# Order and number of loads, held gather numbers and deeper buffers in a two-layer transformer with mixtures of experts

## The chip, the cores and the metric

The kernel runs on one core of a Trainium2 chip, as one launch. The metric is device time in microseconds (us) of that core, as the median of several runs. A core has five engines that work side by side, each on its own queue of instructions: TensorE (PE in the profile; its weight loads are listed as PEld), VectorE (DVE), ScalarE (ACT), GpSimd (POOL) and SyncE (SP). SP only issues transfers (DMAs); ACT and POOL can issue some too. An engine takes its instructions strictly in order, so an instruction that waits for a semaphore holds everything behind it on that engine.

## The reference, cut to what matters

Eight sequences of 512 tokens with 256 numbers each pass through two pre-norm blocks, each an attention and a mixture of experts:

```python
x = x + _L0_attn_ref(_layernorm(x), Wq, Wk, Wv, Wo)          # 16 heads of 16, 4 key heads, rotary, causal
x = x + _L0_ffn_ref(_layernorm(x), router_w, w_gate, w_up, w_down)
x = x + _L1_attn_ref(_layernorm(x), w_qkv, b_qkv, w_out, b_out)
x = x + _L1_ffn_ref(_layernorm(x), gate_w, w1, w2, w3, sw1, sw2, sw3)
```

The first mixture has 32 experts with 96 inner numbers, of which each token takes the 8 likeliest, with their weights normed to one. The second has 16 experts with 176 inner numbers, of which each token takes 2, and a shared expert with 352 inner numbers that every token passes through. An expert is the same in both:

```python
h = jax.nn.silu(x @ wg) * (x @ wu)
acc = acc + h @ wd * w_e[:, None]
```

All numbers are float32.

## The kernel before, in words

**Stages.** The program runs through four stages: attention 0 (to about 417 us), mixture 0, or MoE 0 (to about 871), attention 1 with the shared expert (to about 1427) and MoE 1 (to the end). In an attention stage a pipeline works on sequence after sequence. At the end of a sequence `route` chooses the experts and POOL scatters the normed rows of its tokens, each chosen token once for each of its experts, into a table `xg` in DRAM that is ordered by expert (L401). A row carries the numbers, the expert weights and the row number to which its result goes.

**Experts.** A MoE stage is run by `all_experts` (L1352) and `experts` (L1078). The sequences are split into two parts with tables of their own (`SPLIT`: four and four in MoE 0, six and two in MoE 1), so that the first part can start while the last sequences are still routed. A job is two tiles of 128 rows. There are 75 jobs a part in MoE 0, and 30 and 14 in MoE 1. Each job passes through five stages at fixed lags of whole steps: `load` (SP fetches the rows into `xg_m`, L1113, 7 buffers, lag 0), `turn_x` (TensorE transposes them into `xgT`, VectorE copies them to `xgTs`, L1122 and L1124, lag 4), `gate_up` (matmuls `gu`, L1155, ACT's SiLU, VectorE's product `h`, L1147, lag 5), `turn_h` (transposes `hT`, copy `hTs`, L1175 and L1176, lag 6) and `down` (matmuls `y`, L1186, lag 7). TensorE's order in it is the written order; the other engines' instructions are placed by a scheduler, which works with priorities and modelled times while the program is built.

**Results of a job.** ACT copies `y` to `ys` (L1191, 4 buffers). In MoE 0 SP stores `ys` in the table's own order (L1193). In MoE 1 POOL scatters it to the rows of its tokens (L1197), two scatters a job, for which VectorE takes the row numbers out of the loaded rows into a small tile `to` (L1132 to L1135, 5 buffers) at the start of `gate_up`.

**Weights.** The gate and up weights are loaded during the attention before. The down weights `dw` are loaded by `load_down` (L1255 to L1264), which `all_experts` calls ahead of `experts`: one transfer for each expert or piece of one that lies in one block of 128 rows, 48 in MoE 0 and 52 in MoE 1. They all stand on SP's queue.

**Work beside the jobs.** `Beside` runs other work a few steps at a time between the jobs. In MoE 0 that is the table of part 1, the weights of the next attention and, once part 0 is done, `gathers` (L1214) for sequences 0 to 3. `gathers` computes on VectorE the rows in which a token's eight results lie (`ykey` L1220 and L1221, `ykeys` L1224, `yrows` L1226), then POOL fetches them and adds them to `x_a` (L1229, 32 transfers a sequence). Sequences 4 to 7 are gathered during attention 1. In MoE 1 it is `results` (L1286): x comes back from DRAM as `x_c` (L163), two gathered tiles `g` (L1294) are added to it (L1305), TensorE transposes it (`xout`, L1315), ACT copies it to `xo` (L1316, one buffer) and SP stores it (L1317).

**x between stages.** A ring of five x tiles holds sequences in work (`new_x`). `keep_x` (L160) stores a sequence to DRAM, `fetch_x` (L163) brings it back. After attention 1 all eight are stored, the last by `x_kept` (L1388).

**The start.** `fast0` (L805) begins attention 0. On ACT's queue stand the loads of the q weights (L810), then the k weights (L819), cos and, behind the copy of the k weights, the v weights and sin (L830). SP has the identity, the router's weights `rw` and the biases (L201 to L204), and then x of sequence 0 (L1269). `issue_after(a)` lets the scheduler place an instruction only behind `a`.

Of the kernel before, what the change touches and what calls it, by code (L numbers as in the profile page):

```python
# [1 line left out]

# [5 lines left out]
F32 = mybir.dt.float32  # L8
# [82 lines left out]
def two_blocks_kernel(  # L91
# [106 lines left out]
        yield  # L198

    rw = cpool.tile([P, ND * (E0 + E1)], F32, tag="rw", name="rw")  # L200
    nc.sync.dma_start(out=rw[:, : ND * E0], in_=r0)  # L201
    nc.sync.dma_start(out=rw[:, ND * E0 :], in_=r1)
    bias1 = cpool.tile([P, BBW], F32, tag="bias1", name="bias1")
    nc.sync.dma_start(out=bias1, in_=b1)  # L204


    tpool = ctx.enter_context(tc.tile_pool(name="tiles", bufs=1, reuse_waits="tile"))
# [595 lines left out]
        return v1[:, t, : heads * (DH + 1)].rearrange("p (h d) -> p h d", d=DH + 1)[:, :, :DH]  # L803

    def fast0(awp, lnp, atp, late, ptp, ps, bank):  # L805
        ahead = {0: read_x(0, lnp)}
        wq = awp.tile([P, ND, D + 2 * HKV * DH], F32, tag="wqkv", name="wqkv0")
        lo, hi = A0["q"]
        q_in = lnp.tile([P, hi - lo], F32, tag="xT", name="q_in")
        nc.scalar.dma_start(out=q_in, in_=a0[:, lo:hi])  # L810
        q_in = q_in.rearrange("p (k m s g r) -> p k m s g r", k=ND, m=2, s=2, g=NG)
        for k in range(ND):
            q_out = wq[:, k, :D].rearrange("p (m g s d) -> p m g s d", m=2, g=NG, s=2)
# [261 lines left out]
            for item in self.items:  # L1075
                drain(item[3])

    def experts(n, gu, dn, mp, ps, again, beside):  # L1078

        name = f"m{n}{'g' * again}"  # L1080
        jobs = [(lay, i) for lay in lays[n] for i in range(0, lay.tiles(again), 2)]
# [45 lines left out]
        def gate_up(lay, i):  # L1127
            part = lay.part
            xT, xg = made.pop(("xT", part, i)), made.pop(("xg", part, i))
            h = mp.tile([P, 2, inner], F32, tag="h", name=f"h_{name}_{part}_{i}")  # L1130
            if n:
                to = made["to", part, i] = mp.tile([P, 2], I32, tag="to", name=f"to_{name}_{part}_{i}", bufs=5)  # L1132
                for j in range(2):

                    nc.vector.tensor_scalar(  # L1135
                        to[:, j : j + 1], xg.bitcast(I32)[:, j, D + lay.n_e :][:, bass.ds(offs[part, i + j][2], 1)],
                        -1.0, None, ALU.add,
                    )
            if n == 0:
                whole = ps.tile([P, 2, 2 * inner], F32, tag="gu", name=f"gu_{name}_{part}_{i}")  # L1140
                gus = [whole[:, 0, :], whole[:, 1, :]]
            else:
                gus = [ps.tile([P, 2 * inner], F32, tag="gu", name=f"gu_{name}_{part}_{i + j}") for j in range(2)]

            def scaled(j):

                nc.vector.scalar_tensor_tensor(  # L1147
                    h[:, j, :], h[:, j, :], xg[:, j, D:][:, bass.ds(offs[part, i + j][2], 1)], gus[j][:, inner:],
                    ALU.mult, ALU.mult,
                )  # L1150

            for j in range(2):
                at = offs[part, i + j][0]
                for c in range(ND):
                    nc.tensor.matmul(  # L1155
                        gus[j], xT[:, j, c, :], gu[:, bass.ds(at + c * 2 * inner, 2 * inner)],
                        start=(c == 0), stop=(c == ND - 1),
                    )
# [20 lines left out]
        def down(lay, i):  # L1179
            part = lay.part  # L1180
            hT = made.pop(("hT", part, i))
            y = ps.tile([P, 2, D], F32, tag="y", name=f"y_{name}_{part}_{i}")
            for j in range(2):
                at = offs[part, i + j][1]
                for q, (lo, n_in) in enumerate(chunks):
                    nc.tensor.matmul(  # L1186
                        y[:, j, :], hT[:n_in, q, j, :], dn[:n_in, bass.ds(at + q * D, D)],
                        start=(q == 0), stop=(q == n_ch - 1),
                    )
            ys = mp.tile([P, 2, D], F32, tag="ys", name=f"ys_{name}_{part}_{i}", bufs=4)  # L1190
# [16 lines left out]
        with tc.manual_schedule(engines={ENG.PE}):  # L1207
            for s in range(len(jobs) + stages[-1][1]):
                for stage, lag in stages:
                    if 0 <= s - lag < len(jobs):  # L1210
                        stage(*jobs[s - lag])
                beside.step(s)
            beside.finish()

    def gathers(b, gat, again=""):

        lay = lay_of(0, b)
        n_e, k, name = lay.n_e, lay.k, f"{again}_{b}"
        key = gat.tile([P, NT, n_e], F32, tag="ykey", name=f"ykey{name}", bufs=1)
        nc.vector.tensor_tensor(key, lay.keys[b], lay.shift.unsqueeze(1).to_broadcast([P, NT, n_e]), ALU.add)  # L1220
# [34 lines left out]
    def load_down(w, src, inner, routed):  # L1255

        chunks = -(-inner // P)
        width = inner // chunks
        for n, lo, hi, e, at in pieces(inner, routed):
            while lo < hi:  # L1260
                q, r = at // width, at % width
                rows = min(hi - lo, width - r)
                to = (e * chunks + q) * D
                nc.sync.dma_start(out=w[r : r + rows, to : to + D], in_=src[n][lo : lo + rows, 2 * ND * P :])  # L1264
                lo, at = lo + rows, at + rows

    def read_x(b, tmp, bufs=1):
        xf = tmp.tile([P, ND, T], F32, tag="xf", name=f"xf{b}", bufs=bufs)
        nc.sync.dma_start(out=xf, in_=x_in[b])  # L1269
        return xf  # L1270

    def load_x(b, tmp, bank, xf=None):
# [12 lines left out]
    def results(seqs, gat, op, ps, again="", behind=lambda: None):  # L1285


        def begin(b):
            fetch_x(b, x_after[1], f"c1{again}")
            lay = lay_of(1, b)  # L1290
            made[b] = [gat.tile([P, NT, D], F32, tag="gath", name=f"g1{again}_{b}_{i}", bufs=2 * K1) for i in range(K1)]
            for i in range(K1):
                lo = (i * len(lay.seqs) + b - lay.seqs[0]) * T
                nc.sync.dma_start(out=made[b][i], in_=lay.yg[lo : lo + T, :].rearrange("(p t) d -> p t d", t=NT))  # L1294
                yield
# [3 lines left out]
        for b, after in zip(seqs, [*seqs[1:], None]):  # L1299
# [11 lines left out]
            for c in range(ND):  # L1311
# [2 lines left out]
                for t in range(NT):  # L1314
                    nc.tensor.transpose(tr[:, t * P : (t + 1) * P], xs[b][:, t, c * P : (c + 1) * P], ident)  # L1315
                nc.scalar.copy(xf[:, c, :], tr)  # L1316
            nc.sync.dma_start(out=out[b], in_=xf)  # L1317

    def drain(part):
        for _ in part:  # L1320
# [32 lines left out]
    def all_experts(n, gw, gat, again=False, weights=()):  # L1353
# [6 lines left out]
        with ExitStack() as s:  # L1360
# [3 lines left out]
            ps = s.enter_context(tc.tile_pool(name=f"ps_m{n}{g}", bufs=2, space=PSUM, reuse_waits="tile"))  # L1364
            inner, chunks, src, routed = (I0, 1, f0, N0) if n == 0 else (I1, ND1, f1, N1R)
            dw = dwp.tile([P, lays[n][0].n_e * chunks * D], F32, tag="dw", name=f"dw{n}{g}")
            load_down(dw, src, inner, routed)

            def bank(name):
                return ps.tile([P, T], F32, tag="y", name=name)  # L1370
# [1 line left out]
            def x_in_ring():  # L1372
                for b in range(SPLIT[0]):
                    fetch_x(b, x_after[0], f"a1{g}")
                yield
                for b in range(SPLIT[0]):
                    yield from gathers(b, gat, g)

            def x_kept():
                with tc.issue_after(beside.load):  # L1380
                    keep_x(NB - 1, x_after[n])
                yield

            def weights_loaded():
# [7 lines left out]
            end = first + second + 6  # L1392
            beside = Beside()
            beside.add(2, min(34, first - 4), 6 + lays[n][1].n_e // 8, tables(lays[n][1], small, bank, again, beside))
            if not again:
                beside.add(8, 9, 1, x_kept())
            beside.add(
                first // 2, end, len(weights), weights_loaded(),
# [1 line left out]
            if n == 0:  # L1400
                beside.add(done, end, SPLIT[0] * 16 + 1, x_in_ring())
            else:
                beside.add(
                    done + 2, end, SPLIT[1] * 6, results(range(SPLIT[1]), gat, gat, ps, g, lambda: beside.last)
                )
            experts(n, gw, dw, mp, ps, again, beside)
            return beside.last


# [26 lines left out]
    with ExitStack() as s1:  # L1436
# [4 lines left out]
        with ExitStack() as s:  # L1441
# [15 lines left out]
            def after1(b):  # L1457
# [3 lines left out]
                xT = yield from turned(xn, lnp, bank, name)  # L1461
                yield from route(1, b, xn, xT, name, False)
                yield from shared(w1["s"], xT, xs[b], name)
                if b < NB - 1:
                    keep_x(b, x_after[1])
                if b == SPLIT[1] - 1:
                    yield from tables(lays[1][0], smp, bank, False)
# [38 lines left out]
    def general1(gat):  # L1506
        with ExitStack() as s:
# [20 lines left out]
            def all_of(b, name):  # L1528
# [8 lines left out]
                keep_x(b, x_after[1])  # L1537

            for b in range(NB):
                drain(all_of(b, f"f1g_{b}"))  # L1540
# [175 lines left out]
```

## Time and profile before

| What | Value |
|---|---|
| Median of 3 runs | 1705.02 us (1702.58 to 1710.43) |
| The profiled execution | 1707.52 us |
| Its span | 1705.8 us |
| Mean granted clock of TensorE | 0.962 |
| Scatters of rows to the experts (POOL, L401) | 320, 321.5 us busy |
| Gathers of MoE 0's results (POOL, L1229) | 256, 403.8 us busy |
| Gate and up matmuls (PE, L1155) | 1552, 339.1 us busy |
| Down matmuls (PE, L1186) | 952, 238.4 us busy |
| Loads of job rows (SP, L1113) | 388 of 144 KB |
| Bytes read and written in DRAM | 133.42 and 125.37 MB |

Times of the profile are counted from the start of the span. A row such as `start, length, engine, line, operation, out<-in xN` stands for N instructions of one kind that follow each other on their engine. What stands in brackets behind it is how long the engine had been idle before the first, and what ended that. A profile is of one execution, and its own time stands beside its span.

### The profile page before, as it was taken

The numbers are of one execution on the slowest core, as the hardware profiler recorded it, in microseconds if no ns is written. First come the engines' busy times: TensorE is split into PE (matmuls) and PEld (weight loads), VectorE is DVE, ScalarE is ACT, GpSimd is POOL, SyncE is SP. The second block draws the span as 40 slices with busy tenths as digits, with TensorE's granted clock in tenths as the row PEclk, the third lists the DMA queues.
The fourth block names the chain that finished last, engine by engine and source line by source line (L and its number), as shares of the span: only waits on it lengthen the run. The fifth ranks groups of instructions, "written<-read, shape, count | busy, mean of one in ns | idle before, by whom it ended". The sixth has DMA issues, their size and how long they took to land.

```text
span 1705.8 us, 31140 instructions
## 1 busy us (share of the span) xinstructions
PE 1551.6 (91%) x10180; PEld 1034.3 (61%) x10180; DVE 995.5 (58%) x3179; ACT 650.1 (38%) x865; POOL 822.4 (48%) x686
## 2 busy tenths in 40 slices
PE   5899999994999999999989999999899989999884
PEld 2355544543898999899863454544444445777663
DVE  5687887875555555555555765754656544444353
ACT  2555554552232333333334454454455331222222
POOL 0026777477710003888888548888511012333333
PEclk9999999997899999999999999999999999999997
DMA  2035557236988768999985345665312025353353
GB/s 73 13 87 155 163 166 269 97 138 197 303 255 259 212 200 216 265 274 274 275 188 71 44 109 80 128 139 72 84 53 84 25 92 168 99 160 106 120 186 143
DMA packets 246618, 257.84 MB, mean 151 GB/s; under 512 B 80907, under 2 KB 225425, under 8 KB 246452
## 3 DMA queue, kind: packets, MB, share of 16 engines
q1 hardware_dynamic: 189508, 165.73, 32.1%
q0 software_dynamic: 56448, 89.18, 22.6%
q8 instruction: 87, 1.43, 0.4%
q10 hardware_dynamic: 496, 0.85, 0.2%
q14 instruction: 79, 0.65, 0.1%
HBM read 133.42 MB, written 125.37 MB: 152 GB/s over the span
## 4 chain that ended last, share of the span: by engine, by line
PE 47%; POOL 19%; issue 14%; DVE 10%; DMA 5%; ACT 2%; SPq 2%; POOLq 0%; DVEq 0%; ACTq 0%
POOL x_a L1229 15%; PE gu_m L1155 7%; PE st_a L654 7%; PE o_a L677 6%; PE y_m L1186 4%; PE qkv_a L859 3%; PE xgT_m L1122 2%; POOL yg L1197 2%; PE sg_f L418 2%; POOL xg L401 2%; ACT p_a L659 2%; DVE p_a L665 2%; PE y_a L743 2%; PE su_f L418 2%; PE sy_f L431 2%
## 5 line engine op out<-in xcount | busy, mean ns | idle before, releaser
L1229 POOL DMA_INDIRECT x_a<-yg,yrows x256 | 403.8, 1577 | 279.9 <-DMA xg_m<-xg 184.5
L401 POOL DMA_INDIRECT xg<-xn_f,rows_f x320 | 321.5, 1005 | 413.7 <-DVE xn_f L396 177.6
L659 ACT ACTIVATE p_a<-st_a 128x2048 f32<-128x2048 f32 (+1 forms) x192 | 306.0, 1594 | 277.9 <-PE st_a L654 243.0
L1155 PE MATMUL gu_m<-gw,xgTs_m 128*128 x1552 | 339.1, 362 | 13.2 <-DVE h_m L1147 10.1
L1155 PEld LDWEIGHTS gu_m<-gw,xgTs_m 128*128 128x128 f32 x1552 | 259.2, 193 | 46.1 <-DVE h_m L1147 12.5
L1186 PE MATMUL y_m<-dw,hTs_m 96*128 (+1 forms) x952 | 238.4, 380 | 0.0
L654 PE MATMUL st_a<-qT_a,kT_a 32*128 32x512 f32 (+3 forms) x2048 | 200.9, 476 | 11.2 <-ACT p_a L659 11.0
L677 PE MATMUL o_a<-p_a,v 128*32 128x512 f32 (+3 forms) x2048 | 197.8, 455 | 6.3 <-DVE p_a L665 6.1
L665 DVE TENSOR_TENSOR p_a<-p_a,causal 128x512 f32<-128x512 f32 x256 | 170.5, 684 | 55.8 <-ACT p_a L659 54.8
L1191 ACT COPY ys_m<-y_m 128x512 f32<-128x512 f32 x194 | 113.6, 585 | 188.7 <-PE y_m L1186 169.9
L1124 DVE COPY xgTs_m<-xgT_m 128x512 f32<-128x512 f32 x194 | 133.5, 688 | 77.4 <-PE xgT_m L1122 77.3
L1186 PEld LDWEIGHTS y_m<-dw,hTs_m 96*128 96x128 f32 (+1 forms) x952 | 165.8, 190 | 15.2
L1197 POOL DMA_INDIRECT yg<-ys_m,to_m x88 | 94.0, 1068 | 167.8 <-ACT ys_m L1191 153.2
L1147 DVE SCALAR_TENSOR_TENSOR h_m<-h_m,xg_m,gu_m 128x96 f32<-128x96 f32 (+1 forms) x388 | 113.8, 326 | 86.8 <-ACT h_m L1160 46.3
L654 PEld LDWEIGHTS st_a<-qT_a,kT_a 32*128 32x128 f32 x2048 | 89.6, 188 | 106.3 <-issue 50.5
L1176 DVE COPY hTs_m<-hT_m 96x256 f32<-96x256 f32 (+1 forms) x194 | 92.9, 479 | 102.3 <-PE hT_m L1175 102.0
L1122 PE MATMUL xgT_m<-ident,xg_m 128*128 128x128 f32 x776 | 120.6, 277 | 19.9 <-DMA xg_m<-xg 13.3
L1163 ACT ACTIVATE h_m<-gu_m 128x192 f32<-128x192 f32 x150 | 49.5, 330 | 212.9 <-PE gu_m L1155 200.3
L1122 PEld LDWEIGHTS xgT_m<-ident,xg_m 128*128 128x128 f32 x776 | 96.7, 143 | 44.3 <-issue 15.9
L677 PEld LDWEIGHTS o_a<-p_a,v 128*32 128x32 f32 x2048 | 49.6, 110 | 108.1 <-issue 66.9
L1175 PE MATMUL hT_m<-ident,h_m 128*96 128x128 f32 (+1 forms) x476 | 84.4, 274 | 0.0
L683 DVE COPY osb_a<-o_a 128x512 f32<-128x512 f32 x64 | 44.0, 688 | 53.3 <-PE o_a L677 53.3
(202 smaller groups left out, 1698.6 us busy)
## 6 DMA issues: line engine op xcount, KB each, us to landing
xg_m<-xg SPq DMA_DIRECT2D x388, 144.0 KB
yg<-ys_m SPq DMA_DIRECT2D x150, 256.0 KB
xg<-zeros SPq DMA_DIRECT2D x100, 144.0 KB
g<-yg SPq DMA_DIRECT2D x16, 512.0 KB
xg<-xn_f,rows_f POOLq DMA_INDIRECT x320
xf<-in_x_dram SPq DMA_DIRECT2D x8, 512.0 KB
x_after<-x_in SPq DMA_DIRECT2D x8, 512.0 KB
x_a<-x_after SPq DMA_DIRECT2D x8, 512.0 KB
```

Source lines behind the costliest of these rows:

```text
L401: inst = nc.gpsimd.indirect_dma_start(out=lay.xg, out_offset=bass.IndirectOffsetOnAxis(ap=rows[:, t, i : i + 1], axis=0), in_=xn[:, t, :], ...
L654: nc.tensor.matmul(st[:, g, at : at + T - j * P], kT[r, j * P : (j + 1) * P], qT[r, j * P :], start=True, stop=True,)
L659: nc.scalar.activation(pt, st[:, :, :width], AF.Exp, scale=SCALE)
L665: self.masked = nc.vector.tensor_tensor(d, d, causal.unsqueeze(1).to_broadcast([P, NG, P]), ALU.mult).ins
L677: nc.tensor.matmul(o[32 * g : 32 * g + 32, j * P :], v1[:, j, v_at + g * (DH + 1) :][:, :32], probs[n][:, g, at : at + T - j * P], start=( ...
L1122: nc.tensor.transpose(tr[:, j, c, :], xg[:, j, c * P : (c + 1) * P], ident)
L1124: nc.vector.tensor_copy(xT, tr)
L1147: nc.vector.scalar_tensor_tensor(h[:, j, :], h[:, j, :], xg[:, j, D:][:, bass.ds(offs[part, i + j][2], 1)], gus[j][:, inner:], ALU.mult, A ...
L1155: nc.tensor.matmul(gus[j], xT[:, j, c, :], gu[:, bass.ds(at + c * 2 * inner, 2 * inner)], start=(c == 0), stop=(c == ND - 1),)
L1186: nc.tensor.matmul(y[:, j, :], hT[:n_in, q, j, :], dn[:n_in, bass.ds(at + q * D, D)], start=(q == 0), stop=(q == n_ch - 1),)
L1197: inst = nc.gpsimd.indirect_dma_start(out=lay.yg, out_offset=bass.IndirectOffsetOnAxis(ap=to.bitcast(U32)[:, j : j + 1], axis=0), in_=ys[: ...
L1229: nc.gpsimd.indirect_dma_start(out=xs[b][:, t, :], out_offset=None, in_=lay.yg[: lay.tiles(bool(again)) * P, :], in_offset=bass.IndirectOf ...
```

## The change

The parts of the change, in the order of the stages:

- Attention 0 begins with x of sequence 0, loaded in two halves of 256 tokens. The q weights follow on SP's queue, no longer on ACT's, and then the router's weights and the biases (`load_small`).
- The numbers of the gathers of sequences 0 to 3 are computed behind `beside.last`, the latest `hTs` copy of the experts at that point.
- `load_down` is called inside `experts`, at step 3, when the loads of jobs 0 to 3 have been written. A transfer takes the same piece of every group of experts whose rows stand alike in blocks of 128: 6 transfers in MoE 0 and 26 in MoE 1.
- In MoE 1 `to` has 12 buffers and `ys` has 8.
- Sequences 6 and 7 stay in the ring between attention 1 and the results; they are neither stored nor fetched. x of the others comes back into three buffers of the gathers' pool. `x_kept` is left for MoE 0 alone.
- `results` starts two steps earlier and takes seven steps a sequence instead of six. The outputs of sequences 6 and 7 are stored in two halves.

```diff
+    def load_small():
+        nc.sync.dma_start(out=rw[:, : ND * E0], in_=r0)
+        nc.sync.dma_start(out=rw[:, ND * E0 :], in_=r1)
+        nc.sync.dma_start(out=bias1, in_=b1)
...
-        ahead = {0: read_x(0, lnp)}
+        ahead = {0: read_x(0, lnp, NT // 2)}
...
-        nc.scalar.dma_start(out=q_in, in_=a0[:, lo:hi])
+        nc.sync.dma_start(out=q_in, in_=a0[:, lo:hi])
+        load_small()
...
-                to = made["to", part, i] = mp.tile([P, 2], I32, tag="to", name=f"to_{name}_{part}_{i}", bufs=5)
+                to = made["to", part, i] = mp.tile([P, 2], I32, tag="to", name=f"to_{name}_{part}_{i}", bufs=12)
...
-            ys = mp.tile([P, 2, D], F32, tag="ys", name=f"ys_{name}_{part}_{i}", bufs=4)
+            ys = mp.tile([P, 2, D], F32, tag="ys", name=f"ys_{name}_{part}_{i}", bufs=4 + 4 * n)
...
+                if s == 3:
+                    load_last()
                 beside.step(s)
...
-    def gathers(b, gat, again=""):
+    def gathers(b, gat, again="", behind=None):
...
-        nc.vector.tensor_tensor(key, lay.keys[b], lay.shift.unsqueeze(1).to_broadcast([P, NT, n_e]), ALU.add)
+        with tc.issue_after(behind) if behind else ExitStack():
+            nc.vector.tensor_tensor(key, lay.keys[b], lay.shift.unsqueeze(1).to_broadcast([P, NT, n_e]), ALU.add)
...
-        for n, lo, hi, e, at in pieces(inner, routed):
+        whole = math.lcm(inner, P)
+        again = routed // whole
+        src = src[: routed // P].rearrange("(a n) p c -> n p a c", a=again)
+        w = w.rearrange("p (a x) -> p a x", a=again)
+        for n, lo, hi, e, at in pieces(inner, whole):
...
-                nc.sync.dma_start(out=w[r : r + rows, to : to + D], in_=src[n][lo : lo + rows, 2 * ND * P :])
+                nc.sync.dma_start(out=w[r : r + rows, :, to : to + D], in_=src[n, lo : lo + rows, :, 2 * ND * P :])
...
-    def read_x(b, tmp, bufs=1):
-        xf = tmp.tile([P, ND, T], F32, tag="xf", name=f"xf{b}", bufs=bufs)
-        nc.sync.dma_start(out=xf, in_=x_in[b])
+    def read_x(b, tmp, tiles=NT):
+        xf = tmp.tile([P, ND, T], F32, tag="xf", name=f"xf{b}", bufs=1)
+        for lo in range(0, T, tiles * P):
+            nc.sync.dma_start(out=xf[:, :, lo : lo + tiles * P], in_=x_in[b, :, :, lo : lo + tiles * P])
...
-            fetch_x(b, x_after[1], f"c1{again}")
+            if b < SPLIT[1]:
+                xs[b] = gat.tile([P, NT, D], F32, tag="x", name=f"x_c1{again}_{b}", bufs=3)
+                nc.sync.dma_start(out=xs[b].rearrange("p t d -> p (t d)"), in_=x_after[1][b])
+                yield
...
-            nc.sync.dma_start(out=out[b], in_=xf)
+                if b >= SPLIT[1]:
+                    nc.sync.dma_start(out=out[b, :, c, :], in_=xf[:, c, :])
+            if b < SPLIT[1]:
+                nc.sync.dma_start(out=out[b], in_=xf)
...
-            load_down(dw, src, inner, routed)
...
-                    yield from gathers(b, gat, g)
+                    yield from gathers(b, gat, g, beside.last)
...
-                    keep_x(NB - 1, x_after[n])
+                    keep_x(NB - 1, x_after[0])
...
-            if not again:
+            if n == 0 and not again:
                 beside.add(8, 9, 1, x_kept())
...
-                    done + 2, end, SPLIT[1] * 6, results(range(SPLIT[1]), gat, gat, ps, g, lambda: beside.last)
-                )
-            experts(n, gw, dw, mp, ps, again, beside)
+                    done, end, SPLIT[1] * 7, results(range(SPLIT[1]), gat, gat, ps, g, lambda: beside.last)
+                )
+            experts(n, gw, dw, mp, ps, again, beside, lambda: load_down(dw, src, inner, routed))
...
-                if b < NB - 1:
+                if b < SPLIT[1]:
                     keep_x(b, x_after[1])
```

More of the change, by code (lines that the diff above doesn't have):

```diff
@@ L1 @@
+import math
 from contextlib import ExitStack
@@ L200, in two_blocks_kernel @@
     rw = cpool.tile([P, ND * (E0 + E1)], F32, tag="rw", name="rw")
-    nc.sync.dma_start(out=rw[:, : ND * E0], in_=r0)
-    nc.sync.dma_start(out=rw[:, ND * E0 :], in_=r1)
     bias1 = cpool.tile([P, BBW], F32, tag="bias1", name="bias1")
-    nc.sync.dma_start(out=bias1, in_=b1)
+    def load_small():
+        nc.sync.dma_start(out=rw[:, : ND * E0], in_=r0)
+        nc.sync.dma_start(out=rw[:, ND * E0 :], in_=r1)
+        nc.sync.dma_start(out=bias1, in_=b1)
     tpool = ctx.enter_context(tc.tile_pool(name="tiles", bufs=1, reuse_waits="tile"))
@@ L1076, in finish, with experts @@
                 drain(item[3])
-    def experts(n, gu, dn, mp, ps, again, beside):
+    def experts(n, gu, dn, mp, ps, again, beside, load_last):
         name = f"m{n}{'g' * again}"
@@ L1536, in all_of @@
                 yield from shared(sw1, xT, xs[b], name)
-                keep_x(b, x_after[1])
+                if b < SPLIT[1]:
+                    keep_x(b, x_after[1])
             for b in range(NB):
```

## The prediction

> **What bounds the kernel now.** I read the page from the top: engine shares, the 40 slices, then the list of waits and the timeline at each place where TensorE stops. The first parts of the page say which engine has to be kept fed:
>
> ```profile
> PE 1551.6 (91%) x10180; PEld 1034.3 (61%) x10180; DVE 995.5 (58%) x3179; ACT 650.1 (38%) x865; POOL 822.4 (48%) x686
> ...
> PE   5899999994999999999989999999899989999884
> ```
>
> TensorE is busy for 1551.6 of 1705.8 us, so all its pauses are about 154 us, and an edit helps only where it shortens one. The page's slices show where to look: the first, the tenth (384 to 426 us) and the last two. The change adds no work to TensorE; it can win in those pauses and in slow clock behind them, and lose by making new ones.
>
> The tenth slice is the seam between attention 0 and MoE 0. Timeline, columns start, duration, engine, instruction, idle before:
>
> ```profile
> 395.65 26.11 SPq L1264 DMA_DIRECT2D dw<-in_f_dram  x48
> 422.63 7.25 SPq L1113 DMA_DIRECT2D xg_m<-xg  x11
> ```
> ```profile
> 426.24 1.09 PE L1122 MATMUL xgT_m<-ident,xg_m 128*128 128x128 f32 x4 [8.72 <-DMA xg_m<-xg]
> ```
>
> SP issues 48 loads of down weights for 26.11 us (0.54 each), and only then the rows of the first tiles, which land when TensorE has waited 8.72 us. The rows themselves were ready: they are sequences 0 to 3, routed long before.
>
> The second place is MoE 1, from 1428 to 1681. The list of waits (total, times, longest), then the timeline at the longest:
>
> ```profile
> DVE to_m L1135 <- DMA yg<-ys_m,to_m: 61.8, 19, 7.1
> ```
> ```profile
> 1606.15 0.28 DVE L1135 TENSOR_SCALAR to_m<-xg_m 128x1 int32 x2 [6.80 <-DMA yg<-ys_m,to_m]
> ...
> 1607.44 4.71 PE L1155 MATMUL gu_m<-gw,xgTs_m 128*128 x8 [4.30 <-DVE h_m L1147]
> ```
>
> A `to` tile (the row numbers of a scatter) has 5 buffers. VectorE may not write the next before an old scatter has landed, and behind it in VectorE's queue stand the copy of xgT and the products h, for which TensorE waits. The eight matmuls after that pause take 4.71 us, against 2.53 for the same eight at 1598.00: a long pause is paid again in clock.
>
> **The change part by part.** All sums are against the profiled execution, 1707.5 us, 2.5 above the median of the runs.
>
> *The start.* The chain of waits begins with two loads on ACT's queue:
>
> ```profile
> 1.73 4.01 DMA cosf<-in_a_dram
> ...
> 6.49 4.26 DMA sinf<-in_a_dram
> ```
>
> q_in leaves that queue, so k_in and cosf move up one place (0.45 us of issue each). v_in at 5.91 waits for the k_in copy, which stood behind four q_in copies (5.12 to 5.74) and now stands first; sinf follows v_in. I take 0.6 us, between 0.3 and 1.0. What SP issues before x moves behind it: x now comes in two halves first, then q_in, rw, bias. q_in becomes the third load of SP (about 1.7 instead of 0.82), but its copies are wanted only at the projections after 18 us.
>
> *Numbers of gathers.* VectorE computes all 24 operations for sequences 0 to 3 (5.1 us) in the middle of the last sequence of attention 0:
>
> ```profile
> 400.80 0.28 DVE L1220 TENSOR_TENSOR ykey<-key,shift 128x128 f32<-128x128 f32 x1
> 401.00 0.68 DVE L747 TENSOR_TENSOR x_in<-x_in,y_a 128x512 f32<-128x512 f32 x1
> ```
>
> Ahead of TensorE's wait there (5.49 us before 407.55) lies a serial chain of otok, x_in, statistics and xn_f on VectorE. Counting only numbers that stand directly in front of a link of it gives about 0.3 + 0.4 + 0.3 = 1.0 us; no less than 0.3, no more than 1.6. In the changed program's order they stand behind the hTs copies of part 1's jobs 5, 23, 41 and 59. So the first gather can no longer start when part 0's results have landed (663.69 before, which would be about 9 earlier now) but some 5 jobs of 2.95 us after them: about 667. What is queued behind it on POOL: 128 gathers at 1.85 us, 32 of sequence 4 (they ended at 959), then the scatter of attention 1's first sequence at 979.87. 959 + 3.5 = 962.5, against 979.87 − 10 = 970: hidden by 7 us, and lost one for one beyond. The later sequences' numbers come every 53 us, their gathers take 59, so they add nothing.
>
> *MoE 0's seam.* In the changed program's order the down weights still stand ahead of the first rows on SP: what falls is their number, 48 to 6, each of up to 96 x 8 runs of 1 KB. No row shows such a transfer. Nearest rows: 128 runs cost SP 0.33 us, the store of ys with 256 runs 0.39. In line with that 768 runs cost 0.6, six 3.6 us; at worst, cost in proportion to runs, 2.0 each, 12 us. So the rows are issued at about 400 (at worst 408). But the weights' bytes stay ahead of them: 3.15 MB. Here the Trainium skill speaks against the change ("DMA: Bandwidth & Descriptors", Queues, rings and completion order): each DMA engine consumes its ring in order, so an earlier issue doesn't overtake what is queued. Trace, columns window, length, busy PE, PEld, DVE, ACT, POOL, clock, DMA share, GB/s:
>
> ```profile
> 415.00:420.00 5.00, 1.03 (x8) 0.53 (x8) 3.77 (x28) 0.84 (x1) 3.84 (x4) 0.50 0.75 234
> 420.00:425.00 5.00, 0.00 (x0) 0.00 (x0) 0.00 (x0) 0.00 (x0) 3.83 (x4) 0.50 0.72 217
> ...
> 429.00:431.00 2.00, 2.00 (x8) 2.00 (x9) 0.69 (x1) 0.00 (x0) 1.69 (x2) 0.50 1.00 344
> ```
>
> While SP issued, the DMA engines were 0.75 busy at 234 GB/s; at full share they moved 344. Beside POOL's scatters (147 KB every 1.26 us, 117 GB/s) some 227 stay: 3.15 MB take 13.9 us, and the rows land near 395.65 + 2 + 13.9 = 411.6. By the skill's ceiling in its section Bandwidth (435 GB/s for the ports) it would be 7.2 us, 405; if the rate stayed at 120 GB/s as before, 422 to 424. I take the row. TensorE ends the routing at 417.52 either way, so the wait goes unless the rate doesn't rise. What is late next is VectorE: its last routing operation ends at 419.22, then the xgTs copy of 0.69; the first gate matmuls start at about 420.3 instead of 429.39. Gain 9.0, at worst 2.
>
> Does the clock add to this? The skill ("TensorE: Matmul & The Clock Gate", Part 1) gives half rate after some 3.4 us without work and full rate after as much work, so a lost wait of 8.72 us would also save an estimated 1.7 us of half-rate matmuls. But the rows above show 0.50 already before the wait, since TensorE paused until 407.55. The ramp is merely paid earlier; I add nothing.
>
> *MoE 1.* With 12 buffers no `to` waits for a scatter of the last jobs. Pauses in front of gate matmuls that go with it: 0.58 + 0.60 + 0.59 + 1.39 + 0.37 + 0.60 + 0.61 + 4.30 + 0.81 = 9.9. Results, spread one transpose group and two adds a step instead of bunched: pauses of 2.26, 2.85 and 1.17 become half, 3.1. Clock: two bursts of eight at 4.71 and 4.22 instead of 2.53 are 3.9; with long pauses gone I count 3. Against that, a **new wait**: VectorE now has `to` of a job that is seven ahead, whose rows were issued right after h freed their tile. Latency is 2.2 us (median in MoE 1; nine tenths under 2.7), the second row goes out 0.54 after the first, so `to` can run 2.7 to 3.2 us after that h; the next h comes 3.4 after it. Mostly hidden; I charge 0.05 a job, 2 us, and 1 us at the change of parts, where SP's result loads wait for scatters ahead of the last rows. Sum 9.9 + 3.1 + 3 − 3 = 13, from 5 (half the pauses return) to 20 (the granted clock of 0.93 from 1580 to 1681 goes to 1.00 as well). The 52 loads become 26 and end before 1411; TensorE begins at 1428: nothing. The x of sequences 6 and 7 stays on chip: four 512 KB transfers that nobody waited for: nothing.
>
> *The tail.* After the last matmul of y:
>
> ```profile
> 1692.32 1.95 PE L1315 MATMUL xout<-ident,x_c 128*128 128x128 f32 x8 [11.29 <-DVE x_c L1305]
> 1694.91 4.59 SPq L1317 DMA_DIRECT2D out_dram<-xo  x2
> ```
>
> Scatter, gather, adds stay serial. Stores by halves let the first half leave 0.8 us earlier and the last be 256 KB, and the copies no longer wait for a whole store (1698.07): 1.2 us, 0 to 2.5.
>
> **Sum:** 0.6 + 1.0 + 9.0 + 13 + 1.2 = 24.8. 1707.5 − 24.8 = 1682.7; against the median, 1705.0 − 24.8, **1680**.
>
> **Rivals.**
>
> *Half comes back* (0.16). The removed wait of `to` is replaced by one for rows, and tight buffers for xo keep the result pauses: MoE 1 gives 3 instead of 13, total 14.8, 1690. For it: the loads are issued only just in time. Against: 0.7 us of slack a job.
>
> *The rows are not ahead* (0.10). The order still has the weights first; if they move at 120 GB/s, MoE 0 gives 2 and the total is 17.8, 1687. For it: the order. Against: DMA share 0.75 with SP issuing back to back.
>
> *Slower* (0.05): VectorE stalls for rows in every job of MoE 1. It decides from a latency of about 3.4 − 0.54 + x: at x = 0.6 a job, 44 jobs cost 26 us and eat the gain; at 3.7 us latency (x = 0.84) it costs 37, 1680 + 37 = 1717. For it: the longest latency there is 4.75. Against: nine in ten are under 2.7.
>
> *More* (0.08): MoE 1 runs at full clock without a pause, 20 us, and the seam gives 10.5: 1671.
>
> *The forecast* has 0.61, its own range 1673 to 1687.
>
> **How the numbers follow.** A measurement of this kernel can tell about 0.5% (8.5 us) from no change: faster is below 1696.5. Forecast, the better case, the rows' case (0.79 together) and most of the half case (0.10 of 0.16) give 0.89; within 0.5%, 0.06; slower, 0.05. The range reaches from the better case with a little room, 1667, to the sum of the low ends (0.3 + 0.3 + 2 + 5 + 0 = 7.6, so 1697); what is left out is the slower case and the edges of the half case, under 2 in 10.
>
> **What would show it.** The first xgT of MoE 0 follows the routing within 1 us, and six dw issues take 3 to 5 us in SP's row. The `to` waits name xg instead of yg and sum to less than 20 us. TensorE's idle time from 1428 on falls from 17.5 to 6 or so at a clock near 1.00. The first x_a gather starts near 667. I am wrong if the gate matmuls still pause in front of h, if the rows land after 420, or if attention 1 has new pauses in front of x_a.

## The result and the profile after

| | Before | Changed |
|---|---|---|
| Median | 1703.80 us (4 runs) | 1680.63 us (4 runs, 1675.96 to 1684.63) |
| Ratio to before | | 0.9856, 95% interval 0.9816 to 0.9895 |
| Profiled execution, span | 1705.8 us | 1676.6 us |
| Mean granted clock | 0.962 | 0.966 |

The change takes 1.4% off; the predicted 1680 is met to 0.6 us, which is partly luck (below). The profiled execution of the changed kernel (1678.4 us) is a little below its median, that of the kernel before a little above, so the pair of spans differs by 29.2 us where the medians differ by 23.2. The table sorts those 29.2 by stage, each from the last instruction of the stage before. It holds the prediction's terms, which by no means all agree:

| Stage | Before | After | Gain | Predicted |
|---|---|---|---|---|
| First xT_a starts | 17.96 | 16.65 | 1.3 | 0.6 |
| From there to the end of routing in attention 0 | 399.56 | 398.48 | 1.1 | 1.0 |
| End of routing to the first gate matmul | 11.87 | 5.44 | 6.4 | 9.0 |
| From there to the last y of MoE 0 | 441.50 | 438.10 | 3.4 | 0 |
| To the first xgT of MoE 1 | 557.26 | 560.69 | -3.4 | 0 |
| MoE 1, first xgT to last y | 252.45 | 231.88 | 20.6 | 13 |
| Tail | 25.20 | 25.35 | -0.1 | 1.2 |

Which of these rows are the change and which are chance is what the experiments are for. First the lines that answer to those shown of before. The page:

```profile
PE 1543.9 (92%) x10180; PEld 1030.3 (61%) x10180; DVE 995.9 (59%) x3179; ACT 650.3 (39%) x865; POOL 819.5 (49%) x686
...
PE   5899999996999999999988999998899997999994
```

TensorE's busy time falls by 7.7 us although it does the same 10180 matmuls: they ran at a higher clock. The rest is pauses. The tenth slice goes from 4 to 6. The timeline there, SP and then TensorE:

```profile
393.55 4.10 SPq L1279 DMA_DIRECT2D dw<-in_f_dram  x6
398.47 30.65 SPq L1117 DMA_DIRECT2D xg_m<-xg  x18
```
```profile
414.65 0.48 PE L382 MATMUL rk_f<-before_f,ones 128*128 128x32 bf16 x2
418.69 1.94 PE L1126 MATMUL xgT_m<-ident,xg_m 128*128 128x128 f32 x8 [3.56 <-issue]
420.56 2.93 PE L1159 MATMUL gu_m<-gw,xgTs_m 128*128 x8
```

Six transfers take SP 4.10 us where 48 took 26.11; the rows go out from 398.47 on. The first of these 18 issues is slow:

```profile
398.47 3.92 SPq L1117 DMA_DIRECT2D xg_m<-xg  x1
```

It takes 3.92 us, where the issue of a row takes 0.33 as a rule (and 0.37 behind the 48 loads before). So SP is held until 402.39, not 397.65. By the trace's landing events the last weights land at 411.78 and the first two loads of rows at 411.96 and 412.70: behind the last of the weights, as their place in the queue says, and still ahead of the end of routing at 415.13. Yet TensorE pauses for 3.56 us, and the profile names no other engine and no transfer ("issue"). In TensorE's own queue there stand four loads of registers from `offi` (the offsets of the experts, L1100), which the views don't list since register instructions don't count as busy. Their records begin at 414.94 and last 0.78, 0.90, 0.87 and 0.69. They stood there before too, under the wait for rows.

In MoE 1, TensorE's waits in front of the gate matmuls before (total, times, longest), then two lines of the list of waits after, then two rows of the windows of each (window, length, busy PE, PEld, DVE, ACT, POOL, then granted clock, DMA share and GB/s), before first:

```profile
PE gu_m L1155 <- DVE h_m L1147: 10.1, 10, 4.3
```
```profile
DVE to_m L1139 <- DMA xg_m<-xg: 32.0, 30, 7.0
...
PE gu_m L1159 <- DVE h_m L1151: 2.8, 1, 2.8
```
```profile
1580.00:1610.00 30.00, 25.09 (x115) 18.67 (x114) 11.71 (x31) 5.58 (x14) 10.01 (x11) 0.91 0.43 142
...
1630.00:1680.59 50.59, 42.47 (x200) 31.65 (x199) 26.52 (x57) 12.99 (x29) 21.58 (x15) 0.93 0.49 169
```
```profile
1571.00:1601.00 30.00, 27.01 (x133) 20.34 (x133) 13.68 (x35) 6.93 (x17) 10.19 (x11) 1.00 0.51 166
...
1621.00:1651.24 30.24, 29.22 (x149) 22.06 (x148) 17.34 (x32) 9.27 (x20) 12.99 (x11) 1.00 0.53 181
```

`to` waits for the rows now and no longer for scatters, in 30 places, 32.0 us. TensorE loses 2.8 us to it, once, at the change of parts. And the clock, which had been down to 0.91 and 0.93 over the last hundred microseconds, is 1.00. TensorE's pauses in MoE 1 fall from 17.5 us to 4.2, its busy time from 234.9 to 227.7: 13.3 and 7.2 make the 20.6 but for roundings.

The tail hardly moves:

```profile
1662.61 1.94 PE L1334 MATMUL xout<-ident,x_a 128*128 128x128 f32 x8 [10.93 <-DVE x_a L1324]
```

### The profile page after: what moved, and what is told of

It reads as the page before. It is cut to its first block, busy times and chain, and to the rows that moved or that the text cites. A ratio compares the mean times of both kernels' runs of the same rounds, so it can differ in the third digit from the quotient of the medians.

```text
span 1676.6 us, 31034 instructions
## 1 busy us (share of the span) xinstructions
PE 1543.9 (92%) x10180; PEld 1030.3 (61%) x10180; DVE 995.9 (59%) x3179; ACT 650.3 (39%) x865; POOL 819.5 (49%) x686
## 3 DMA queue, kind: packets, MB, share of 16 engines
q0 software_dynamic: 56448, 89.18, 23.2%
## 4 chain that ended last, share of the span: by engine, by line
PE 69%; DVE 10%; POOL 8%; issue 5%; DMA 4%; ACT 3%; SPq 1%; DVEq 0%; POOLq 0%; ACTq 0%
PE gu_m L1159 17%; PE y_m L1190 11%; PE st_a L657 7%; PE o_a L680 6%; POOL x_a L1239 6%; PE xgT_m L1126 5%; PE hT_m L1179 3%; PE qkv_a L863 2%; PE sg_f L421 2%; ACT p_a L662 2%; PE sy_f L434 2%; PE su_f L421 2%; POOL xg L404 2%; DVE p_a L668 2%; PE y_a L746 2%
## 5 line engine op out<-in xcount | busy, mean ns | idle before, releaser
L1159 PE MATMUL gu_m<-gw,xgTs_m 128*128 x1552 | 334.1, 359 | 2.9 <-DVE h_m L1151 2.8
L1201 POOL DMA_INDIRECT yg<-ys_m,to_m x88 | 88.9, 1010 | 151.9 <-ACT ys_m L1195 137.3
```

Source lines behind the costliest of these rows:

```text
L1159: nc.tensor.matmul(gus[j], xT[:, j, c, :], gu[:, bass.ds(at + c * 2 * inner, 2 * inner)], start=(c == 0), stop=(c == ND - 1),)
```

## The experiments

Theory A is the prediction with what the trace pair added: the number of dw transfers made MoE 0's wait; what is left of it is TensorE's register loads; `to` made most of MoE 1's gain. The expectations name its rivals.

**Number or order.** The load of the down weights was changed in two ways at once: fewer transfers, and a later place in the program (which the scheduler did not follow: they still stand ahead of the rows). Three kernels separate these. The first undoes the number:

```diff
-        for n, lo, hi, e, at in pieces(inner, whole):
+        for n, lo, hi, e, at in pieces(inner, routed):
...
-                nc.sync.dma_start(out=w[r : r + rows, :, to : to + D], in_=src[n, lo : lo + rows, :, 2 * ND * P :])
+                nc.sync.dma_start(out=w[r : r + rows, to : to + D], in_=src[n][lo : lo + rows, 2 * ND * P :])
```

> The changed kernel with the down weights in 48 and 52 transfers again, at the same place of SP's queue (ahead of the rows). Theory A (the number of transfers made the wait): TensorE's pause between the last routing matmul and the first xgT of MoE 0 goes from 3.56 back to 8 to 9 us, SP issues dw for about 26 us; time 4 to 6 us above the changed kernel's 1680.6, so 1685 to 1687. Rival B (the load's new place in the program, not the number, made it): the pause stays under 4 us and the time at 1680.

Its timeline:

```profile
389.97 26.30 SPq L1274 DMA_DIRECT2D dw<-in_f_dram  x48
```
```profile
420.40 1.09 PE L1126 MATMUL xgT_m<-ident,xg_m 128*128 128x128 f32 x4 [8.85 <-DMA xg_m<-xg]
```

The pause is back at 8.85 us and is again put down to the rows; from the end of routing to MoE 0's last y it takes 451.9 us against 443.5. The number of transfers is the cause, and rival B falls. The whole time doesn't show it: 1681.69, ratio 0.9882 (0.9838 to 0.9925), 1 us above and not 4 to 6. Attention 0 ended at 411.55 in this execution, 3.6 earlier than in the changed kernel's; the changed kernel and its variants spread over 411.5 to 419.8 there, so that a single time is not the place to look for 5 us.

The second kernel holds the weights behind the rows:

```diff
                 if s == 3:
-                    load_last()
+                    with tc.issue_after(beside.load):
+                        load_last()
```

> The changed kernel with the down weights held behind the rows of job 3, so that the rows of the first tiles really stand ahead on SP's queue. Theory A (in the changed kernel the rows had landed at 412.7, before TensorE ended the routing at 415.1, and the pause of 3.56 is its own four register loads): pause unchanged at 3.4 to 3.7 us, the first y not later than 429, time 1679 to 1682. Rival B (the rows behind 3.15 MB of weights set the pause): pause under 2 us, time 2 us less.

The pause is 3.22 us and MoE 0 takes 442.6 from the end of routing: close to theory A, and not under 2 as rival B has it. The first y starts at 425.64. SP's row:

```profile
401.20 7.65 SPq L1280 DMA_DIRECT2D dw<-in_f_dram  x6
```

Here the six issues take 7.65 us, not 4.10, and the row issued behind them another 4.63. Time 1676.61, ratio 0.985 (0.9826 to 0.9873). Rows that are really ahead bring nothing that can be told, because they were in time already.

The third also holds the weights back, and has 48 and 52 transfers again:

> Rows first, and 48 and 52 transfers. If order alone is enough, as theory A has it: pause 3.4 to 3.7 us as with few transfers, dw issued from about 400 to 426, first y at 428 to 430, time 1679 to 1683. Rival C (the long row of dw issues then holds up the rows of later jobs or the weights come late for y): a pause of 1 us or more in front of a y or of an xgT in the first 40 us of MoE 0, time 1684 or more.

```profile
399.77 2.92 SPq L1117 DMA_DIRECT2D xg_m<-xg  x6
402.74 27.90 SPq L1275 DMA_DIRECT2D dw<-in_f_dram  x48
```
```profile
433.21 2.05 PE L1190 MATMUL y_m<-dw,hTs_m 96*128 x4 [6.33 <-DMA dw<-in_f_dram]
```

Rival C is right here and theory A is wrong. The pause in front of the rows is 3.29, but the long row of issues now makes the weights late for the first y, 6.33 us. MoE 0 takes 448.2, the time is 1683.25, ratio 0.9882 (0.9844 to 0.992). Order alone only moves the wait from the rows to the weights; the number removes it.

**The rest of that wait.** The loads of the offsets' registers are written behind the transposes of a job's rows:

```diff
-            at = [
+            for j, row in enumerate(v):
+                rows[lay.part, i + j] = row
+
+        def offsets(lay, i):
+
+            at = [
...
             made["xT", part, i] = xT
+            if i % RB == 0:
+                offsets(lay, i)
```

> The changed kernel with TensorE's and VectorE's loads of expert offsets written behind the transposes of a job's rows and not at the load of the rows, so that no register load stands in front of the first xgT. Theory A (the four register loads of 0.69 to 0.90 us on TensorE's queue are the pause): the pause falls from 3.56 to under 0.7 us, two register loads (1.7 us) then stand behind the first xgT, partly under the copy to xgTs; first gate matmul 2 to 3 us earlier against the end of routing; time 1677 to 1679. Rival B (the pause is the routing's end on VectorE or the rows): pause stays above 2.5 us, time 1680.

```profile
420.49 1.09 PE L1131 MATMUL xgT_m<-ident,xg_m 128*128 128x128 f32 x4 [0.65 <-PE rk_f L382]
422.58 1.09 PE L1131 MATMUL xgT_m<-ident,xg_m 128*128 128x128 f32 x4 [1.00 <-DMA xg_m<-xg]
```

The pause falls to 0.65, which shows that it was the register loads (two of them now stand behind the first xgT, from 420.54 to 422.52), and the first gate matmul comes 3.62 us after the end of routing, not 5.44. From the end of routing MoE 0 takes 440.0, where the changed kernel took 443.5 and the others here with few transfers and the held numbers 442.4 to 444.3. Yet the time is 1682.11, ratio 0.9876 (0.9853 to 0.9899): no gain, where 1677 to 1679 was expected. In this build the scheduler also placed instructions of attention 0 in another order, from its seventh sequence on; attention 0 ended at 419.84, the latest of all, and attention 1 took 563.7. Whether that is the build or the execution is open.

**MoE 1.** One edit on the kernel before (`to` with 12 buffers, not 5), and the changed kernel without it and with 4 buffers for `ys`:

```diff
-                to = made["to", part, i] = mp.tile([P, 2], I32, tag="to", name=f"to_{name}_{part}_{i}", bufs=5)
+                to = made["to", part, i] = mp.tile([P, 2], I32, tag="to", name=f"to_{name}_{part}_{i}", bufs=12)
```

> The kernel before with one edit: 12 buffers for to. Theory A (the waits for old scatters carry most of MoE 1's gain, in pauses and in the clock behind them): MoE 1 from the first xgT to the last y goes from 252.4 to 238 to 243 us; pauses in front of gate matmuls sum to under 4 us, the longest at the change of parts; time 1690 to 1695. Rival D (the spread of the results made the gain): MoE 1 stays at 247 or more, time 1699 or more.

```diff
-                to = made["to", part, i] = mp.tile([P, 2], I32, tag="to", name=f"to_{name}_{part}_{i}", bufs=12)
+                to = made["to", part, i] = mp.tile([P, 2], I32, tag="to", name=f"to_{name}_{part}_{i}", bufs=5)
...
-            ys = mp.tile([P, 2, D], F32, tag="ys", name=f"ys_{name}_{part}_{i}", bufs=4 + 4 * n)
+            ys = mp.tile([P, 2, D], F32, tag="ys", name=f"ys_{name}_{part}_{i}", bufs=4)
```

> The changed kernel with 5 buffers for to and 4 for ys again, the results as changed. Theory A: VectorE's to waits for scatters (yg) again, 40 us or more in all; MoE 1 goes from 231.9 to 241 to 247 us; time 1690 to 1696. Rival D: MoE 1 at 236 or less, time under 1685.

These two were timed together with two more that follow and with the kernel before, and all five took some 300 us longer than elsewhere (the kernel before 2000.39), most of it in attention 0, with waits that the profile puts down to "remote"; what that was is open. So of these four kernels neither the times nor the sums of stages up to attention 1 are used, and only MoE 1 is read: its first part took 142.37 us in the two that have all of the change in MoE 1, to the hundredth as in the changed kernel elsewhere.

`to` alone: MoE 1 takes 238.87 us, inside its range, 13.6 less than before, and its first part 142.91 against 148.65. The list names the rows and no longer the scatters:

```profile
DVE to_m L1135 <- DMA xg_m<-xg: 37.4, 35, 6.4
```

TensorE's pauses fall from 17.5 to 8.4 us, those in front of gate matmuls from 10.1 to 3.1, and its busy time from 234.9 to 230.5. With the results as changed but `to` with 5 buffers, MoE 1 takes 263.86 us. That is above the 241 to 247 expected, and above the kernel before (252.45). The reason stands in the list of waits and in the second part:

```profile
DVE to_m L1139 <- DMA yg<-ys_m,to_m: 58.6, 19, 9.3
...
PE xout L1334 <- DVE x_c L1324: 10.7, 3, 6.1
```
```profile
1911.28 0.29 DVE L1139 TENSOR_SCALAR to_m<-xg_m 128x1 int32 x2 [6.78 <-issue]
...
1912.77 1.28 DVE L1324 TENSOR_TENSOR x_c<-x_c,g 128x512 f32<-128x512 f32 x2
...
1913.60 1.20 PE L1334 MATMUL xout<-ident,x_c 128*128 128x128 f32 x4 [6.12 <-DVE x_c L1324]
```

VectorE stands at a `to` for 6.78 us (the profile names no releaser for this one; 19 others are put down to scatters, 58.6 us). Behind it in its queue are h, hTs and the adds of x_c, and TensorE now has one transpose group of results after almost every y, so it waits for those adds three times, up to 6.12 us. The results as changed cost 11.4 us as long as `to` has 5 buffers, and bring 7.0 (238.87 to 231.88) once it has 12. Rival D is wrong, and so is a sum that gives each of the two a gain of its own. `ys` had 4 buffers in the one case and 8 in the other, and the results have their spread, their own buffers for x and the x kept on chip; these were not tried apart.

**The numbers held.** `beside.last` is not given to `gathers`:

```diff
-                    yield from gathers(b, gat, g, beside.last)
+                    yield from gathers(b, gat, g)
```

> The changed kernel with the numbers of the gathers not held. The prediction's step: TensorE's wait in front of the last xT_f of attention 0 grows by 0.3 to 1.0 us from 5.30, nothing else; time 1 us above. What the trace pair suggests instead (theory E): that wait grows by only 0.2 us, but the numbers of sequences 4 to 7 come back to the first jobs of MoE 0 and make a pause of about 3 us there with slow clock behind it; MoE 0 from the end of routing is 2 to 5 us longer than 443.5; the first gather starts when part 0 has landed, about 10 us earlier in the stage, and attention 1 is no shorter for it; time 1682 to 1686.

This is one of the four disturbed kernels. What it still shows is a pause of 2.96 us at 63 us after the end of routing, which the two of them with the hold don't have. The same edit in undisturbed runs:

> The numbers of the gathers not held, once more, because in the earlier call engines stood still in attention 0 for reasons outside the kernel. Theory E: the wait in front of the last xT_f is 5.3 to 5.7 us against 5.30; a pause of about 3 us near 35 us after the end of routing, slow clock behind it; MoE 0's first part 4 to 6 us longer than the control's, its second part 0 to 2 us shorter; the first gather 8 us earlier in part 1, attention 1 the same within 2 us; time 2 to 5 us above the control. The prediction's step alone: 1.0 us, all of it in front of xT_f.

The control is the changed kernel itself, timed together with it:

> The changed kernel itself, as the control for the others on this chip: ratio to the kernel before 0.984 to 0.988; MoE 1 from first xgT to last y 231 to 233 us, its first part 142.4; the pause in front of MoE 0 3.2 to 3.6 us.

The control has 1675.48 us, ratio 0.9837 (0.9812 to 0.9863), MoE 1 232.01, a pause of 3.82 in front of MoE 0. Without the hold it is 1679.69, 0.9853 (0.9825 to 0.9882); the intervals overlap, so the whole time doesn't settle it. The wait in front of the last xT_f is 5.44, against 5.00 in the control and 5.30 to 5.34 in the seven other undisturbed kernels with the hold: 0.1, at most 0.4. The rest of theory E stands too:

```profile
443.57 0.18 DVE L1236 TENSOR_SCALAR yrows<-ykeys 128x32 uint32<-128x32 f32 x1
443.67 0.68 DVE L1128 COPY xgTs_m<-xgT_m 128x512 f32<-128x512 f32 x1
...
444.40 2.93 PE L1159 MATMUL gu_m<-gw,xgTs_m 128*128 x8 [3.03 <-DVE xgTs_m L1128]
```

From 438.60 to 443.75 VectorE computes the numbers of sequences 4 to 7 without a break, as soon as part 1's table, from which they are made, is there; the copy of xgT stands behind, TensorE pauses 3.03 us, and its next eight matmuls take 2.93 us, not 1.47. From the end of routing to the first xgT of part 1 it takes 225.15 us against 221.39 in the control, 3.8 less with the hold; the other kernels with few transfers and the hold, registers apart, have 221.6 to 222.5, so 2.7 to 3.8. The second part is 0.1 shorter. The first gather starts 8.1 us earlier in part 1 (13.90 and 21.98 after its first xgT), and attention 1 takes 559.11 against 558.43: those 8 us cost nothing.

**The start** as before, the small loads ahead of x again:

> The changed kernel with the start as before: q weights on ACT's queue, small loads ahead of x, x in one piece. Theory A: the first xT_a starts at 17.9 to 18.0 us instead of 16.65, all else alike, so 1.3 us in the profile, less than what the timing can tell; time 1679 to 1684. Rival F (the earlier start is absorbed by the pipeline): the second sequence's work stands at the same time with and without, within 0.3 us.

The first xT_a starts at 17.58, ahead of the stretch that was disturbed. The three kernels with the old start have 17.25 to 17.96, 17.6 on average, the eleven executions with the new one 15.71 to 17.21, 16.4 on average: 1.2 us earlier, with a scatter as large. Whether it is still there at the end of attention 0 can't be read from the disturbed run, so rival F stays open.

**The tail.** The results spread to two steps before the end, alone and with the rows first:

```diff
-                    done, end, SPLIT[1] * 7, results(range(SPLIT[1]), gat, gat, ps, g, lambda: beside.last)
+                    done, end - 2, SPLIT[1] * 7, results(range(SPLIT[1]), gat, gat, ps, g, lambda: beside.last)
```

> The changed kernel with the results beside MoE 1's jobs spread to two steps before the end, not to the end. Theory G (at the end VectorE's adds of x_c stretch one of POOL's scatters to 3.15 us, and the backlog of scatters sets the tail): the last adds end two jobs earlier, the last scatters follow their y at once, the tail after the last y goes from 25.35 to about 24 us; but two xout groups now stand together in some steps, as before the change, which may cost pauses of 1 us each in front of xout; sum minus 1 to plus 2, time 1679 to 1683. Rival H (the tail is fixed by scatter, gather and adds in series): tail unchanged within 0.4 us.

> Rows first in few transfers, and the results two steps earlier: the two that may beat the changed kernel together. MoE 0 from the end of routing 442.5 to 443.5, tail as the run before it; time between 1676 and 1682, so no difference from the changed kernel that can be told, unless both are real and it stands 2 to 4 us below the changed kernel on the same chip.

POOL's last scatters in the first of the two:

```profile
1645.13 0.98 POOL L1201 DMA_INDIRECT yg<-ys_m,to_m  x1 [0.33 <-ACT ys_m L1195]
...
1649.00 0.99 POOL L1201 DMA_INDIRECT yg<-ys_m,to_m  x1 [0.30 <-issue]
```

None of the last six is stretched any more; in the changed kernel one of them took 3.15 us while VectorE added x_c. Still the tail is 25.04, and 24.29 with the rows first, against 25.35 and the control's 24.45. The last two y's now follow each other directly and end at 1645.95, so that their four scatters queue up in series all the same: the last one starts 3.05 us after the last y has ended (2.81 in the changed kernel). So theory G was about something that didn't set the end here. How far the tail itself moves can't be told: it is 23.6 to 26.5 in undisturbed kernels that leave it as the change has it. With the rows first MoE 0 takes 444.1 us, a little above what was expected. Times: 1675.09, ratio 0.984 (0.9811 to 0.9869), and with the rows first 1679.03, 0.9858 (0.9835 to 0.9881). Neither differs from the control; no version was found that beats the changed kernel by what can be told.

## Why the prediction was right

The mechanisms at the two main places were right; the number was so close because errors of both signs cancelled, and by luck: the same kernel, as the control, stood 28.2 us below the kernel before, not 23.2. Of the signs that were named, two did not come true: the first xgT of MoE 0 followed the routing after 3.56 us, not within 1, and the waits of `to` for rows summed to 32.0 us, not to less than 20. Step by step:

- **The start, 0.6:** the first xT_a comes 1.2 us earlier on average; that any of it reaches the end is not shown.
- **MoE 0's wait goes with the number of transfers: right, and shown** by undoing the number alone. Six issues were put at 3.6 us and took 4.10, but the row behind them took 3.92 more to issue, which the sum didn't have; it was hidden behind the weights' bytes. The rows were put at 411.6 and landed from 411.96 on, from a start 2.1 us earlier, so the weights' rate was 194 GB/s rather than 227 (3.15 MB in the 16.2 us from 2 us after the first issue). The ring order that was set against the change holds in this trace (the last weights landed at 411.78, the first row at 411.96), and cost nothing, as the second load of rows, at 412.70, was still 2.4 us ahead of the end of routing.
- **"Gain 9.0" at that seam: too high by 2.6.** What is late next was named as VectorE's last routing operation and the xgTs copy. It was TensorE's own queue: four register loads of 3.2 us in all, which the sum left out; before, they were hidden under the wait for rows. Moving them made the pause 0.65.
- **The clock at the seam, taken as no gain:** the ramp runs from the first gate matmuls on in both kernels (eight of them take 2.77 us before, 2.93 after, where 1.47 is usual). Half rate saved would have added 1.7; the row that showed 0.50 ahead of the wait was the right one to go by.
- **Numbers of gathers, "1.0 us, in front of xT_f": place wrong, size short.** In front of xT_f they cost 0.1, at most 0.4. (The table's 1.1 for that row fits by chance: the same stretch takes 395.6 to 402.0 us in the kernels that have it in the same order.) The step left out that the numbers of sequences 4 to 7, which the edit doesn't name, stood in MoE 0 at 451 to 456 and move behind those of 0 to 3, with which they share the one buffer of ykey. That was worth 2.7 to 3.8 us of MoE 0's first part. The profile of before showed a pause of 2.95 us there. The later start of the gathers is hidden, as predicted; it was put at 667 and was 659, since MoE 0's first part was 4.9 us shorter and the hold delays the first gather by 8.1 us, less than the sum had.
- **MoE 1, 13: the mechanism right, the size 20.6.** The pauses fell by 13.3 where 10.0 was summed (9.9 + 3.1 less 3 for new waits). The new wait is 2.8 us in one place, as charged. The mis-sized terms are the pauses around the results, which were to become half and went from 7.3 to 1.3, and the clock, 7.2 for 3. The 20 of the better case named this clock. Wrong was the split: the results' 3.1 us are 7.0 behind 12 buffers and a loss of 11.4 behind 5.
- **MoE 1's 26 transfers and the x kept on chip, nothing:** with 52 transfers again MoE 1 took 232.20 us, with 26 it took 231.88 and 232.01. The kept x was not tried alone.
- **The tail, 1.2:** 25.35 against 25.20 here, 23.6 to 26.5 in the other undisturbed kernels with the changed stores: nothing that stands out of the scatter.
- **Attention 1, no change:** 560.69 against 557.26 looked like 3.4 us given back. The control has 558.43 and the run with early results 557.19; between 1355 and 1360 the first profile ran at a granted clock of 0.50. So most of the 3.4 is the execution, not the change; with a single profile of before in undisturbed runs, a loss of a microsecond or two is not excluded.

Of the rivals, "the rows are not ahead" had the order right and the price wrong: the transfers did get faster. "Half comes back" and "slower" needed the wait of `to` for rows to reach TensorE in many jobs; it did in one, for 2.8 us.

## What to carry to other kernels

Undo one part of a change that has several: here two parts that were summed as independent gains are worth 20.6 us together, 13.6 and minus 11.4 alone (the second also with fewer `ys` buffers), because a small tile with too few buffers stops the engine through which the other part's work has to pass. When a wait is removed, look at what else stands on the waiting engine's own queue during it, register loads too, which no busy time shows. And when work is held back behind a point, ask what follows it by a shared buffer: here that part's gain came from numbers that the edit didn't mention.

## What was not expected of the hardware

Six transfers of up to 768 runs of 1 KB took SP 4.10 us to issue, 0.68 each, and 48 of up to 96 runs took 26.11, 0.54 each. But a part of the price comes later: the next issue on the queue took 3.92 us where 0.33 is usual (3.31 in the control), and with the rows first the six took 7.65 themselves and the next 4.63. What SP waits for there is not shown. TensorE's four register loads at the seam take 0.69 to 0.90 us each in its queue. And the same instructions take different times from execution to execution: attention 0, which stands in the same order on TensorE, VectorE and ScalarE in six of these kernels, ended its routing between 411.5 and 418.3 us; how much of this is the granted clock was not taken apart. So in a kernel of this length a gain of 5 us is read from its stage, beside other executions of the same stage, and not from the time.
